# Two-layer convolution kernel: statistics of the third image moved into the first bands of both layers, weights loaded one by one, stores split, inner convolution in one piece

## Chip, cores and metric

The kernel runs on one core of one Trainium2 chip. The metric is the device time of one launch in microseconds. The kernel before took 3856.01 us, the median of three runs (3853.47 to 3856.48).

## What is computed

The input x is 8 images of 256 channels and 64 x 64 pixels, float32. Two layers follow each other, each adding its result to x after a group normalisation over 32 groups:

```
def _gn(v, G=32, eps=1e-5):
    g = v.reshape(B_, G, C_ // G, H_, W_)
    m = jnp.mean(g, axis=(2, 3, 4), keepdims=True)
    s = jnp.var(g, axis=(2, 3, 4), keepdims=True)
    return ((g - m) / jnp.sqrt(s + eps)).reshape(v.shape)
...
    x = x + _L0_conv_ref(_gn(x), ...)
    x = x + _L1_conv_ref(_gn(x), ...)
```

Layer 0 makes, for each pixel, nine tap weights per group of 8 channels, and applies them to a 3 x 3 window of a third map:

```
x1, x2, x3 = conv1x1(x, w1, b1), conv1x1(x, w2, b2), conv1x1(x, w3, b3)     # 32, 32, 256 channels
h = concatenate([x1, unfold3(reflect_pad(x2))])                              # 320 channels
h = relu(bn2(conv1x1(relu(bn1(h)), cw1)))                                    # 32 channels
w = conv1x1(h, cw2, cb2)                                                     # 9 taps x 32 groups
out = einsum('bgskhw,bgkhw->bgshw', unfold3(pad(x3)), w)
```

Layer 1 is the sum of two branches at half weight each. The first is attention of every pixel over its 7 x 7 neighbourhood, with four heads and a position term. The second takes nine depthwise 3 x 3 convolutions, a ReLU and nine more, and sums them with softmax weights over nine maps that a 256 x 2304 matrix (Wfc) makes.

## The kernel before, in words

An image is cut into 8 bands of 8 rows, so there are 64 bands, and 256 channels are two channel tiles of 128 partitions. The two layers are pipelined over bands: layer 0 is AHEAD = 12 bands ahead of layer 1. One loop runs g from -12 to 63. Each g has 8 steps s, and each step calls `advance()` six times. `after(n, f)` emits f n advances later. No scheduler reorders anything: the order in which the instructions are emitted is the order of each engine's queue, and every engine works through its queue in order. A DMA is issued by the queue of SP or ACT, in order with what else stands there.

Layer 0 of one band goes like this.

- The statistics of raw x are taken in `first_stats` (L279): a load of the band into tile xs (L100, one buffer, SP queue) and two bn_stats on VectorE (L287). This runs AHEAD0 = 21 bands ahead of layer 1. When an image's eight bands are done, `scaled_weights` (L292) forms the affine chain: aggregate, group means by a matmul (L242), sc_a on ScalarE (L146, L147), weights scaled (L300, L301), bi_a on VectorE (L273), bias by a matmul (L308).
- `small_maps` (matmul L332) and `write_maps` (ScalarE L347, L351) make x1 and x2 with three shifted copies; GpSimd adds the borders (L357 to L366). `value_maps` (matmul L375, ScalarE L380, store L382) makes x3 and stores it to DRAM; `values_by_group` loads it by group into x3q (L396 to L404, SP queue).
- `hidden_maps`: three activations write hid (L424), three sets of matmuls sum them (L434), and ReLU gives h2n (L441). In bands of g < 0 one accumulation is used. In bands of g >= 0 the matmuls come in two pieces: two thirds at step 4, a copy to h2n by ScalarE, the last third at step 6, an addition by VectorE (L450), and ReLU.
- `tap_weights`: matmul pw (L470); VectorE multiplies one tap with the shifted window into prod (L483); GpSimd adds prod to xg (L491). For g < -1 the taps come in groups of three, of which TensorE sums the third products with an identity matrix (L504), so that GpSimd has six additions per band, and VectorE's `combine` (L511) adds that sum. For g >= -1 GpSimd does all nine additions. xg starts as x, loaded by `x_by_group` (L412).
- `take` (L519) takes the statistics that layer 1 needs, and `keep` (L529) stores the band to DRAM in four DMAs: on ACT's queue when layer 0 runs alone (L525), on SP's otherwise.

Layer 1 of one band (g >= 0) loads rows with halo (L563 to L567), normalises (L572), makes values, queries and keys (L601, L684, L706), stores and reloads values by window (vd, vt; L621 to L643), makes scores (L750), softmax (L764 to L781), transposes (L787), and weighted values (L799). The other branch runs depthwise taps on VectorE (L843, L869) with ScalarE ends (L834, L879), and the matmuls pf (L886) with the exponential ex (L891). GpSimd sums the exponentials (L1106). `dynamic_sum` (L893) adds the two halves (L899), applies a limit (L902), VectorE takes the reciprocal (L907), and GpSimd multiplies: tot by rec (L908), oc by tot (L913), and adds to xr, which is stored as the output. The tile oc is written by ScalarE (L879) in `depthwise_end` and has two buffers.

The weights of layer 1 (c2 for pw is among them in the list) are all issued in one go by `layer1_loads` (L191) on ACT's queue between 23 and 28 us: wq, wk, wv, wfc (2 MB), mask, last. Afterwards VectorE scales wv (L200) and subtracts the ninth map's matrix from the other eight in two operations of 2048 columns (L205), called at three times that the main block sets.

Of the kernel before, what the change touches and what calls it, by code (L numbers as in the profile page):

```python
# [10 lines left out]
F32 = mybir.dt.float32  # L11
# [7 lines left out]
P = 128  # L19
# [68 lines left out]
def conv_layers_kernel(ctx: ExitStack, tc: tile.TileContext, ins: dict, out: bass.AP):  # L88
# [14 lines left out]
        return t  # L103


    late = []

    def load(name, shape, src=None, now=True):
        t = const.tile(shape, F32, name=f"c_{name}")
        late.append(lambda: nc.scalar.dma_start(out=t, in_=ins[name] if src is None else src))  # L110
        if now:
            late.pop()()
        return t

    nc.scalar.preload_act_table_set(TABLES)
# [6 lines left out]
    c1 = load("c1", [P, 3, REL])  # L122
    gq = load("gq", [P, P])
    gc = load("gc", [P, NCT, P])
    c2 = load("c2", [P, KK, P], now=False)
    wq = load("wq", [P, NCT, C], ins["wq"].rearrange("(t p) n -> p t n", p=P), now=False)
    wk = load("wk", [P, NCT, C], ins["wk"].rearrange("(t p) n -> p t n", p=P), now=False)
    wv = load("wv", [P, NCT, C], ins["wv"].rearrange("(t p) n -> p t n", p=P), now=False)
    wfc_in = ins["wfc"].rearrange("(t p) k n -> p t k n", p=P)
    wfc = load("wfc", [P, NCT, KK - 1, C], wfc_in[:, :, : KK - 1], now=False)  # L130

    ident = const.tile([P, P], F32, name="ident")
    make_identity(nc, ident)
# [57 lines left out]
    def layer1_loads():  # L191


        last = w1.tile([P, NCT, 1, C], F32, tag="oc", name="last")
        for f in late:
            f()
        nc.scalar.dma_start(out=last, in_=wfc_in[:, :, KK - 1 :])

        def first():
            nc.vector.tensor_scalar(wv, wv, rate1, None, ALU.mult)  # L200

        def difference(kt):
            nc.vector.tensor_sub(wfc[:, kt], wfc[:, kt], last[:, kt].to_broadcast([P, KK - 1, C]))  # L205

        return [first, lambda: difference(0), lambda: difference(1)]

    class Image:
        def __init__(self):  # L210
# [9 lines left out]
    def after(n, f):  # L220
        later.append((place[0] + n, f))
# [118 lines left out]
    def write_maps(b, i, p12, half):  # L340
        im = images[b]
        t, bias = im.x2[i], im.bias
        for u in half:
            r, o = u * R // 2, 64 * u
            for q, (dst, src) in enumerate(((1, 0), (0, 0), (0, 1))):
                n = W - (q != 1)
                nc.scalar.activation(  # L347
                    t[32 * q : 32 * q + 32, r + 1 : r + 1 + R // 2, dst : dst + n],
                    p12[o : o + 32, :, src : src + n], AF.Identity, bias=bias[o : o + 32, 0:1],
                )  # L350
            nc.scalar.activation(  # L351
                t[96:128, r : r + R // 2, :], p12[o + 32 : o + 64], AF.Identity, bias=bias[o + 32 : o + 64, 0:1]
            )
        if half[-1] == 0:
            return

        nc.gpsimd.tensor_copy(t[0:32, 1 : 1 + R, 0:1], t[0:32, 1 : 1 + R, 2:3])  # L357
        nc.gpsimd.tensor_copy(t[64:96, 1 : 1 + R, W - 1 : W], t[64:96, 1 : 1 + R, W - 3 : W - 2])

        if i == 0:  # L360
            nc.gpsimd.tensor_copy(t[0:96, 0, :], t[0:96, 2, :])
        else:
            nc.gpsimd.tensor_copy(t[0:96, 0, :], im.x2[i - 1][0:96, R, :])
            nc.gpsimd.tensor_copy(im.x2[i - 1][0:96, R + 1, :], t[0:96, 1, :])
        if i == NB - 1:
            nc.gpsimd.tensor_copy(t[0:96, R + 1, :], t[0:96, R - 1, :])  # L366
# [46 lines left out]
    def hidden_maps(b, i, alone):  # L413

        im = images[b]
        hids = []
        h2 = h2n[i % 2][:, :, :W]

        def hidden(t):
            n = P if t == 0 else 96
            hid = w0.tile([P, R, W], F32, tag="hid", name=f"hid_{b}_{i}_{t}", bufs=2)
            nc.scalar.activation(  # L424
                hid[:n], im.x2[i][:n, t : t + R, :], AF.Relu, bias=bn1b[:n, t : t + 1], scale=bn1s[:n, t : t + 1]
            )
            hids.append(hid)

        def conv(home, first, last, start, stop):
            ph = home[:, 2 * P : 3 * P].rearrange("p (r c) -> p r c", r=SR)  # L430
            for t in range(first, last):
                n = P if t == 0 else 96
                for q in range(NQR):
                    nc.tensor.matmul(  # L434
                        ph[q * REL : (q + 1) * REL], c1[:n, t], hids[t][:n, q * SR : (q + 1) * SR],
                        start=(t == start), stop=(t == stop),
                    )
            return ph

        def relu(v):  # L440
            nc.scalar.activation(h2, v, AF.Relu, bias=bn2b, scale=bn2s)  # L441

        def one(home):
            ph = conv(home, 0, 2, 0, 1)
            after(1, lambda: hidden(2))
            after(2, lambda: nc.scalar.copy(h2, ph))

        def two(home):
            ph = conv(home, 2, 3, 2, 2)
            after(1, lambda: nc.vector.tensor_add(h2, ph, h2))  # L450
            after(3, lambda: relu(h2))

        hidden(0)
        after(3 if alone else 5, lambda: hidden(1))
        if alone:

            home = ps.tile([P, 4 * P], F32, tag="acc", name=f"ph_{b}_{i}")
            after(7, lambda: conv(home, 0, 2, 0, 2))
            after(8, lambda: hidden(2))
            after(12, lambda: after(4, lambda ph=conv(home, 2, 3, 0, 2): relu(ph)))  # L460
        return [two, one]

    def tap_weights(b, i, u, alone, at):

# [48 lines left out]
        def take():  # L513
            x = im.xg[i]
            if i == 0:
                im.st1 = stat.tile([P, 2 * NB, 6], F32, tag="st1", name=f"st1_{b}")
            for t in range(2):
                v = x[:, t * SHARE // 2 : (t + 1) * SHARE // 2].rearrange("p s r c -> p (s r c)")
                nc.vector.bn_stats(im.st1[:, 2 * i + t, :], v)  # L519
            im.x1[i] = dram.tile([C, BAND], F32, tag="x1", name=f"x1_{b}_{i}")  # L520
            if alone:
                after(9, lambda: keep(nc.scalar))
            else:
                keep(nc.sync)

        def keep(queue):
            for q in range(NQR):
                v = im.xg[i][q * REL : (q + 1) * REL].rearrange("p s r c -> p s (r c)")
                queue.dma_start(out=pieces(im.x1[i], q), in_=v)  # L529

# [344 lines left out]

    def depthwise_end(b, i, ct, acc):

        oc = w1.tile([P, BAND], F32, tag="oc", name=f"oc_{b}_{i}_{ct}")
        nc.scalar.activation(oc, acc.rearrange("p r c -> p (r c)"), AF.Copy, scale=rate2)  # L879
        return oc  # L880

# [11 lines left out]
    def dynamic_sum(b, i, ct, ex, oc):  # L893

        tot = w1.tile([P, BAND], F32, tag="tots", name=f"tot_{b}_{i}_{ct}", bufs=1)
        xr = images[b].xr[i]

        engine = nc.vector if (b, i, ct) == (B - 1, NB - 1, NCT - 1) else nc.gpsimd
        engine.tensor_add(tot, ex[:, 1], ex[:, 0])  # L899


        engine.tensor_scalar(tot, tot, 1.0, 1.0e37, ALU.add, ALU.min)  # L902
        rec = w1.tile([P, BAND // 2], F32, tag="rec", name=f"rec_{b}_{i}_{ct}", bufs=1)

        def quotient(u):
            v = tot[:, u * BAND // 2 : (u + 1) * BAND // 2]
            nc.vector.reciprocal(rec, v)  # L907
            after(1, lambda: engine.tensor_mul(v, v, rec))  # L908

        def weigh():  # L910

            engine.tensor_mul(oc, oc, tot)
            engine.tensor_add(xr[:, ct], xr[:, ct], oc)  # L913
            if ct == NCT - 1:
                after(6, store)

        def store():
            nc.sync.dma_start(
                out=out[b].rearrange("(t p) n -> p t n", p=P)[:, :, i * BAND : (i + 1) * BAND], in_=xr
            )  # L920

        after(9, lambda: quotient(0))
        after(13, lambda: quotient(1))
        after(15, weigh)


    def beside(g, s):
# [73 lines left out]
    def steer(g, s):  # L1001
# [22 lines left out]
    with tc.manual_schedule():  # L1024
# [14 lines left out]
        scaled_weights(0)  # L1039
        for _ in range(32):  # L1040
            advance()
        for n, f in enumerate(layer1_loads()):
            after(4 * STEPS * (3 + n), f)

        pending, before, conv, convs, maps = [], None, None, [], []
        for g in range(-AHEAD, B * NB):
            b, i = divmod(g, NB)
            for s in range(STEPS):
# [5 lines left out]
                if g >= 0:  # L1054
                    nm = f"{b}_{i}_{ct}_{m}"
                    weighted = []
                    if m % 2 == 0:
# [154 lines left out]
```

## Time and profile before

| | |
|---|---|
| profiled execution | 3854.63 us |
| its span, first to last instruction | 3852.8 us |
| median of three runs | 3856.01 us |
| granted TensorE clock, mean | 0.994 |
| TensorE busy | 3756.3 us (97%) |
| VectorE, GpSimd, ScalarE busy | 3434.4 (89%), 3116.8 (81%), 2809.2 us (73%) |
| first score matmul of layer 1 (L750) | at 233.62 us |
| combine (L511) of the first and the ninth band | at 67.89 and 210.52 us |
| busy time per 56.3 us band in mid-run, VectorE, GpSimd, ScalarE | about 52.1, 49, 42.5 us |

The table has two times for a whole run: the profiled execution is one run, and its span leaves out what lies around the first and the last instruction. Engines are named PE (TensorE), PEld (its weight loads), DVE (VectorE), ACT (ScalarE), POOL (GpSimd) and SP; a name with q is the engine's queue while it issues or waits for DMAs. In a row of the timeline the first number is the start, the second the time to the end of the last instruction of the row, x3 says that three like instructions are drawn together, and a bracket says how long the engine was idle before and what ended that. In a row of waits the numbers are the sum in us, how many times, and the longest.

### The profile page before, as it was taken

The page shows a single profiled execution, that of the slowest core. Times are in us where ns is not written, and L with a number is a line of the kernel's source. Part 1 is how long each engine was busy: PE and PEld are TensorE (multiplying, and loading weights), DVE is VectorE, ACT ScalarE, POOL GpSimd, SP SyncE. Part 2 cuts the span into 40 slices and gives each one's busy share as a digit, 9 for nine tenths or more (in the row PEclk, how much of TensorE's full clock was granted, in tenths as well). Part 3 has the DMA queues.
Part 4 walks back from the last instruction along what each step waited for, and adds up shares of the span by engine and source line. Part 5 has one row for each costly group of instructions (what it writes and reads, how often), then busy time and mean ns, then how long its engine had stood idle before and what let it go on. Part 6 is the DMA issues. An engine that isn't in the chain of part 4 may idle for free.

```text
span 3852.8 us, 71646 instructions
## 1 busy us (share of the span) xinstructions
PE 3756.3 (97%) x24620; PEld 2109.9 (55%) x24620; DVE 3434.4 (89%) x7125; ACT 2809.2 (73%) x6770; POOL 3116.8 (81%) x2100
## 2 busy tenths in 40 slices
PE   6889999999999999999999999999999999999998
PEld 3445555555555555555555555555555555555554
DVE  6879999999999999899998999999999899978877
ACT  4457777777777777777777777777777777677776
POOL 4868888888897888888888888888888888855565
PEclk9999999999999999999999999999999999999999
DMA  8764544544444544544544544454544544232221
GB/s 247 210 177 128 142 118 129 151 126 118 133 135 131 145 123 115 148 135 127 136 116 142 142 125 120 126 149 125 136 115 117 138 119 114 74 97 78 79 67 37
DMA packets 438926, 490.14 MB, mean 127 GB/s; under 512 B 62016, under 2 KB 324256, under 8 KB 438304
## 3 DMA queue, kind: packets, MB, share of 16 engines
q1 hardware_dynamic: 421984, 469.79, 44.1%
q10 hardware_dynamic: 16576, 15.76, 1.3%
q8 instruction: 194, 3.18, 0.4%
q14 instruction: 172, 1.41, 0.1%
HBM read 343.76 MB, written 145.10 MB: 127 GB/s over the span
## 4 chain that ended last, share of the span: by engine, by line
PE 81%; POOL 10%; DVE 3%; DMA 2%; ACT 2%; issue 2%; SPq 1%; ACTq 0%; POOLq 0%; DVEq 0%
PE pf L886 39%; PE small L799 6%; PE ptp L787 6%; POOL xg L491 6%; PE pk L706 5%; PE pq L684 5%; PE sco L750 5%; PE p L375 5%; PE pv L601 5%; PE pw L470 2%; POOL ex L1106 2%; PE small L332 1%; DVE prod L483 1%; PE small L434 1%; DMA x<-x3n 1%
## 5 line engine op out<-in xcount | busy, mean ns | idle before, releaser
L886 PE MATMUL pf<-yp,c_wfc 128*128 128x512 f32 x4096 | 1916.8, 594 | 11.3 <-DVE prod L483 6.3
L491 POOL TENSOR_TENSOR xg<-xg,prod 128x1024 f32<-128x1024 f32 x549 | 1199.8, 2185 | 132.5 <-DVE prod L483 103.6
L886 PEld LDWEIGHTS pf<-yp,c_wfc 128*128 128x128 f32 x4096 | 739.6, 190 | 711.4 <-issue 654.7
L1106 POOL TENSOR_TENSOR ex<-ex,ex 128x1024 f32<-128x1024 f32 x384 | 908.8, 2367 | 68.5 <-ACT ex L891 65.0
L891 ACT ACTIVATE ex<-pf 128x512 f32<-128x512 f32 x1024 | 604.0, 590 | 347.9 <-PE pf L886 269.2
L843 DVE SCALAR_TENSOR_TENSOR acc<-yp,c_chan,acc 128x504 f32<-128x504 f32 (+3 forms) x1104 | 775.5, 702 | 63.2 <-ACT acc L834 42.8
L483 DVE SCALAR_TENSOR_TENSOR prod<-pw,c_par,x3q 128x1040 f32<-128x1040 f32 x576 | 732.7, 1294 | 107.9 <-PE pw L470 60.8
L869 DVE SCALAR_TENSOR_TENSOR acc<-hid,c_chan,acc 128x504 f32<-128x504 f32 (+3 forms) x1024 | 751.1, 733 | 18.1
L781 ACT ACTIVATE prob<-prob,tot 128x196 f32<-128x196 f32 x1024 | 412.9, 452 | 242.4 <-DVE tot L779 236.8
L772 ACT ACTIVATE prob<-prob,nmax 128x196 f32<-128x196 f32 x1024 | 458.2, 450 | 101.3 <-DVE nmax L764 101.2
L907 DVE RECIPROCAL rec<-tot 128x256 f32<-128x256 f32 x256 | 445.7, 1741 | 28.3 <-POOL tot L902 27.5
L789 ACT COPY pt<-ptp 112x512 f32<-112x512 f32 x511 | 295.9, 579 | 111.8 <-PE ptp L787 111.8
L764 DVE CUSTOM_DVE_ANT_0 prob<-sco,c_mask 128x196 f32<-128x196 f32 x1024 | 324.8, 355 | 31.0 <-PE sco L750 31.0
L787 PEld LDWEIGHTS ptp<-ident,prob 128*112 128x112 f32 x2044 | 227.3, 133 | 184.4 <-issue 132.7
L787 PE MATMUL ptp<-ident,prob 128*112 128x128 f32 x2044 | 319.5, 279 | 0.0
L908 POOL TENSOR_TENSOR tot<-tot,rec 128x256 f32<-128x256 f32 x254 | 185.8, 732 | 145.7 <-DVE rec L907 139.7
L799 PEld LDWEIGHTS small<-pt,vt 112*64 112x64 f32 x8144 | 258.6, 138 | 79.8 <-issue 60.5
L799 PE MATMUL small<-pt,vt 112*64 112x64 f32 x8144 | 294.2, 225 | 3.3 <-DMA vt<-vd 1.8
L601 PE MATMUL pv<-c_wv,yp 128*128 128x256 f32 x1056 | 253.5, 383 | 1.8 <-ACT yp L572 1.8
L902 POOL TENSOR_SCALAR tot<-tot 128x512 f32<-128x512 f32 x127 | 243.9, 1920 | 11.1
L470 PEld LDWEIGHTS pw<-h2n,c_c 128*128 128x128 f32 x1152 | 175.1, 191 | 139.9 <-issue 115.9
L375 PE MATMUL p<-xc,w3s 128*128 128x512 f32 x512 | 243.3, 598 | 0.0
(136 smaller groups left out, 4656.7 us busy)
## 6 DMA issues: line engine op xcount, KB each, us to landing
vt<-vd SPq DMA_DIRECT2D x512, 112.0 KB
x3q<-x SPq DMA_DIRECT2D x128, 264.0 KB
xc<-in_x SPq DMA_DIRECT2D x64, 512.0 KB
xg<-in_xg SPq DMA_DIRECT2D x64, 512.0 KB
yp<-x SPq DMA_DIRECT2D x128, 256.0 KB
xr<-x SPq DMA_DIRECT2D x64, 512.0 KB
out_x<-xr SPq DMA_DIRECT2D x64, 512.0 KB
xs<-in_x SPq DMA_DIRECT2D x57, 512.0 KB
```

Source lines behind the costliest of these rows:

```text
L483: nc.vector.scalar_tensor_tensor(prod[:, :, :RUN], pw[:, j, :RUN].unsqueeze(1).to_broadcast([P, SHARE, RUN]), par[:, PCB2 + k : PCB2 + k + 1],
L491: nc.gpsimd.tensor_add(im.xg[i], im.xg[i], rows(prod))
L601: nc.tensor.matmul(pv[:, g], yp[:, kt, r : r + 2].rearrange("p r c -> p (r c)"), wv[:, kt], start=(kt == 0), stop=(kt == NCT - 1),)
L772: nc.scalar.activation(prob[:, h, :NKEY], prob[:, h, :NKEY], AF.Exp, bias=nmax[:, h : h + 1], scale=-1.0, accum_out=tot[:, h : h + 1],)
L787: nc.tensor.transpose(ptp[:, h, ch], prob[:, h, ch * CHUNK : (ch + 1) * CHUNK], ident)
L799: nc.tensor.matmul(po[half[h], :, t * TQ : (t + 1) * TQ], im.vt[i + ch, m][:n, t, (2 * ct + h) * HD : (2 * ct + h + 1) * HD], pt[:n, h, ch ...
L843: nc.vector.scalar_tensor_tensor(o, yp[:, ct, ra + dr : rb + dr, ca + dc : cb + dc], chan[:, ct, CW1 + k : CW1 + k + 1], o, ALU.mult, ALU.add,
L869: nc.vector.scalar_tensor_tensor(o, hid[:, ra + dr : rb + dr, ca + dc : cb + dc], chan[:, ct, CW2 + k : CW2 + k + 1], o, ALU.mult, ALU.add,)
L886: nc.tensor.matmul(pf, wfc[:, kt, 2 * m + j, ct * P : (ct + 1) * P], images[b].yp[i][:, kt, PAD : PAD + R], start=(kt == 0), stop=(kt == N ...
L891: nc.scalar.activation(ex[:, j].rearrange("p (r c) -> p r c", r=R), pf, AF.Exp)
L907: nc.vector.reciprocal(rec, v)
L1106: after(4, lambda ex=ex, exb=exb: nc.gpsimd.tensor_add(ex, ex, exb))
```

## The change

Seven edits come together.

1. The third image's x statistics are no longer taken one band at a time for g = -5 to 2. They are taken at steps 1, 4 and 7 of g = 0, 1 and 2. For g < -10 the statistics stand at step 6 instead of 3.
2. Layer 1's loads move to SP's queue and are issued one by one over the bands g = -10 to -5 (wfc in four pieces); c2 is loaded with the first constants on ACT. The scaling of wv and the two differences move to later bands.
3. When layer 0 is alone, two of the four stores of `keep` are issued by SP, two by ACT.
4. For the first two bands of the first image, the second half of the small maps is written by VectorE rather than ScalarE, and the first two value maps are both made at step 1.
5. In bands with g >= 0 the inner convolution is one accumulation at step 6, with ReLU directly from PSUM; the copy and the addition go. hid has three buffers rather than two.
6. oc, and the tile `last` that shares its tag, have one buffer rather than two.
7. In the last band of an image, first channel tile, the limit of `dynamic_sum` is emitted five advances later, so one addition of prod to xg stands ahead of it on GpSimd, and the quotients follow later.

```diff
-        late.append(lambda: nc.scalar.dma_start(out=t, in_=ins[name] if src is None else src))
         if now:
-            late.pop()()
+            nc.scalar.dma_start(out=t, in_=ins[name] if src is None else src)
+        else:
+            late[name] = lambda: nc.sync.dma_start(out=t, in_=ins[name] if src is None else src)
...
-    c2 = load("c2", [P, KK, P], now=False)
+    c2 = load("c2", [P, KK, P])
...
+        def piece(n):
+            kt, k = n // 2, slice(n % 2 * (KK // 2), (n % 2 + 1) * (KK // 2))
+            nc.sync.dma_start(out=wfc[:, kt, k], in_=wfc_in[:, kt, k])
...
-        return [first, lambda: difference(0), lambda: difference(1)]
+        return [
+            (2, late["wq"]), (2, late["wk"]), (3, late["wv"]), (3, late["mask"]),
+            (4, lambda: piece(0)), (5, lambda: piece(1)), (6, lambda: piece(2)), (7, lambda: piece(3)),
+            (6, lambda: nc.sync.dma_start(out=last, in_=wfc_in[:, :, KK - 1 :])),
+            (5, scaled), (8, lambda: difference(0)), (9, lambda: difference(1)),
+        ]
...
+            def put(to, v, o, n):
+                if u and b == 0 and i < 2:
+                    nc.vector.tensor_scalar(to, v, bias[o : o + n, 0:1], None, ALU.add)
+                else:
+                    nc.scalar.activation(to, v, AF.Identity, bias=bias[o : o + n, 0:1])
...
-            hid = w0.tile([P, R, W], F32, tag="hid", name=f"hid_{b}_{i}_{t}", bufs=2)
+            hid = w0.tile([P, R, W], F32, tag="hid", name=f"hid_{b}_{i}_{t}", bufs=3)
...
-        def one(home):
-            ph = conv(home, 0, 2, 0, 1)
-            after(1, lambda: hidden(2))
-            after(2, lambda: nc.scalar.copy(h2, ph))
-
-        def two(home):
-            ph = conv(home, 2, 3, 2, 2)
-            after(1, lambda: nc.vector.tensor_add(h2, ph, h2))
-            after(3, lambda: relu(h2))
+        def inner(home):
+            ph = conv(home, 0, 3, 0, 2)
+            after(1, lambda: relu(ph))
...
+        else:
+            after(14, lambda: hidden(2))
+        return [inner]
...
-                after(9, lambda: keep(nc.scalar))
+                after(9, lambda: keep((nc.scalar, nc.scalar, nc.sync, nc.sync)))
...
-        oc = w1.tile([P, BAND], F32, tag="oc", name=f"oc_{b}_{i}_{ct}")
+        oc = w1.tile([P, BAND], F32, tag="oc", name=f"oc_{b}_{i}_{ct}", bufs=1)
...
+        late = 2 if (i, ct) == (NB - 1, 0) else 0
+        if late:
+            after(5, limit)
+        else:
+            limit()
...
-        after(9, lambda: quotient(0))
-        after(13, lambda: quotient(1))
-        after(15, weigh)
+        after(9 + late, lambda: quotient(0))
+        after(13 + late // 2, lambda: quotient(1))
+        after(15 + late // 2, weigh)
...
+            first = g < 2 - AHEAD
-            if s == (2 if alone else 0):
+            if s == (1 if first else 2 if alone else 0):
...
-            if s == (3 if alone else 1):
+            if s == (1 if first else 3 if alone else 1):
...
-        if s == (3 if g < -1 else 7) and g + AHEAD0 < B * NB:
-            first_stats(*divmod(g + AHEAD0, NB), n=40 if g < -1 else 9)
+        at = (6,) if g < 2 - AHEAD else (3,) if g < -1 else (1, 4, 7) if 0 <= g < 3 else (7,)
+        if s in at and not (g < 0 and g + AHEAD0 >= 2 * NB) and g + AHEAD0 < B * NB:
+            n = 2 * NB + 3 * g + at.index(s) if 0 <= g < 3 else g + AHEAD0
+            if n < 3 * NB or g >= 3:
+                first_stats(*divmod(n, NB), n=40 if g < -1 else 9)
...
-        for n, f in enumerate(layer1_loads()):
-            after(4 * STEPS * (3 + n), f)
+        for n, f in layer1_loads():
+            after(6 * STEPS * n - 9, f)
...
-                        if s in (4, 6) and convs:
+                        if s == 6 and convs:
```

More of the change, by code (lines that the diff above doesn't have):

```diff
@@ L103, in load_x @@
         return t
-    late = []
+    late = {}
     def load(name, shape, src=None, now=True):
         t = const.tile(shape, F32, name=f"c_{name}")
-        late.append(lambda: nc.scalar.dma_start(out=t, in_=ins[name] if src is None else src))
         if now:
-            late.pop()()
+            nc.scalar.dma_start(out=t, in_=ins[name] if src is None else src)
+        else:
+            late[name] = lambda: nc.sync.dma_start(out=t, in_=ins[name] if src is None else src)
         return t
@@ L129, in conv_layers_kernel @@
     wfc_in = ins["wfc"].rearrange("(t p) k n -> p t k n", p=P)
-    wfc = load("wfc", [P, NCT, KK - 1, C], wfc_in[:, :, : KK - 1], now=False)
+    wfc = const.tile([P, NCT, KK - 1, C], F32, name="c_wfc")
     ident = const.tile([P, P], F32, name="ident")
@@ L191, in layer1_loads, with scaled @@
     def layer1_loads():
[L194 to L199, printed above, removed]
+        last = w1.tile([P, NCT, 1, C], F32, tag="oc", name="last", bufs=1)
+        def piece(n):
+            kt, k = n // 2, slice(n % 2 * (KK // 2), (n % 2 + 1) * (KK // 2))
+            nc.sync.dma_start(out=wfc[:, kt, k], in_=wfc_in[:, kt, k])
+        def scaled():
             nc.vector.tensor_scalar(wv, wv, rate1, None, ALU.mult)
@@ L344, in write_maps @@
             r, o = u * R // 2, 64 * u
+            def put(to, v, o, n):
[3 more added lines that the diff above has]
+                    nc.scalar.activation(to, v, AF.Identity, bias=bias[o : o + n, 0:1])
             for q, (dst, src) in enumerate(((1, 0), (0, 0), (0, 1))):
                 n = W - (q != 1)
-                nc.scalar.activation(
+                put(
                     t[32 * q : 32 * q + 32, r + 1 : r + 1 + R // 2, dst : dst + n],
-                    p12[o : o + 32, :, src : src + n], AF.Identity, bias=bias[o : o + 32, 0:1],
+                    p12[o : o + 32, :, src : src + n], o, 32,
                 )
-            nc.scalar.activation(
-                t[96:128, r : r + R // 2, :], p12[o + 32 : o + 64], AF.Identity, bias=bias[o + 32 : o + 64, 0:1]
-            )
+            put(t[96:128, r : r + R // 2, :], p12[o + 32 : o + 64], o + 32, 32)
         if half[-1] == 0:
@@ L460, in hidden_maps @@
             after(12, lambda: after(4, lambda ph=conv(home, 2, 3, 0, 2): relu(ph)))
-        return [two, one]
+        else:
+            after(14, lambda: hidden(2))
+        return [inner]
     def tap_weights(b, i, u, alone, at):
@@ L521, in take, with keep @@
             if alone:
-                after(9, lambda: keep(nc.scalar))
+                after(9, lambda: keep((nc.scalar, nc.scalar, nc.sync, nc.sync)))
             else:
-                keep(nc.sync)
-        def keep(queue):
-            for q in range(NQR):
+                keep((nc.sync,) * NQR)
+        def keep(queues):
+            for q, queue in enumerate(queues):
                 v = im.xg[i][q * REL : (q + 1) * REL].rearrange("p s r c -> p s (r c)")
@@ L899, in dynamic_sum, with limit @@
         engine.tensor_add(tot, ex[:, 1], ex[:, 0])
-        engine.tensor_scalar(tot, tot, 1.0, 1.0e37, ALU.add, ALU.min)
+        def limit():
+            engine.tensor_scalar(tot, tot, 1.0, 1.0e37, ALU.add, ALU.min)
+        late = 2 if (i, ct) == (NB - 1, 0) else 0
[3 more added lines that the diff above has]
+            limit()
         rec = w1.tile([P, BAND // 2], F32, tag="rec", name=f"rec_{b}_{i}_{ct}", bufs=1)
```

## The prediction

> **What bounds the kernel now.** I read the page's busy row and slices first, then the busy time by stretch, then PE's waits, then the timeline of one loop of the stage before layer 1 starts.
>
> ```profile
> PE 3756.3 (97%) x24620; PEld 2109.9 (55%) x24620; DVE 3434.4 (89%) x7125; ACT 2809.2 (73%) x6770; POOL 3116.8 (81%) x2100
> PE   6889999999999999999999999999999999999998
> ```
> ```profile
> 0.00:50.00 50.00, 22.30 (x94) 11.98 (x95) 19.24 (x52) 19.43 (x42) 5.26 (x22) 0.93 0.80 271
> 50.00:100.00 50.00, 39.70 (x206) 19.48 (x205) 45.73 (x39) 22.14 (x40) 38.48 (x28) 0.97 0.82 223
> 100.00:150.00 50.00, 40.08 (x211) 20.57 (x210) 42.31 (x53) 23.20 (x45) 39.64 (x31) 0.94 0.82 224
> 300.00:350.00 50.00, 50.00 (x311) 28.15 (x310) 46.00 (x87) 38.99 (x93) 43.81 (x30) 1.00 0.47 130
> ```
> The columns after the length are busy PE, PEld, DVE, ACT and POOL, then the granted clock, DMA share and GB/s. PE lacks 3852.8 - 3756.3 = 96.5 us in all, and 67 of them lie in the first 300 us: the fill, in which layer 0 runs ahead alone. From 300 us on PE is full. So a gain has two places: a shorter fill, and some 30 us of gaps in bands and tail.
>
> ```profile
> PE ph L434 <- ACT hid L424: 20.5, 13, 2.9
> PE sco_sum L504 <- DVE prod L483: 12.0, 8, 2.7
> PE pf L886 <- DVE prod L483: 6.3, 6, 1.1
> ```
> The first two are the fill's; the third is a gap at each of six image changes. What the fill's loop itself hangs on is in DVE and POOL:
>
> ```profile
> 102.80 1.23 DVE L511 TENSOR_TENSOR xg<-sco_sum,xg 128x1024 f32<-128x1024 f32 x1 [0.66 <-POOL xg L491]
> 104.06 1.29 DVE L519 BATCH_NORM_STATS2 st<-xg 128x6 f32<-128x512 f32 x2
> 105.26 6.15 DVE L483 SCALAR_TENSOR_TENSOR prod<-pw,c_par,x3q 128x1040 f32<-128x1040 f32 x5
> 113.08 3.72 DVE L483 SCALAR_TENSOR_TENSOR prod<-pw,c_par,x3q 128x1040 f32<-128x1040 f32 x3 [1.67 <-PE pw L470]
> 116.72 1.28 DVE L287 BATCH_NORM_STATS2 st<-xs 128x6 f32<-128x512 f32 x2
> ```
> ```profile
> 107.90 11.24 POOL L491 TENSOR_TENSOR xg<-xg,prod 128x1024 f32<-128x1024 f32 x5 [2.14 <-DVE prod L483]
> ```
> From combine to combine is 16.4 us: 5.10 until POOL gets its product (combine 1.23, its statistics 1.29, two products), then five adds, 11.24. The first_stats pair (L287, 1.28) comes after POOL's products are queued, and DVE still waits 0.66 + 1.67 = 2.3 us in the loop. It is beside the path.
>
> **The change part by part.** The sum is against the profiled execution: 3854.6 us, span 3852.8, 1.8 around it. The median shown, 3856.0, is 1.4 above it; the difference is applied to the median.
>
> *Statistics out of layer 0 alone.* Five pairs (1.28 each), their loads on SP and 2.6 MB leave: 0 by the loop above, at most 5 x 1.28 = 6.4 where DVE is the late one. I take 0. One load fewer stands ahead of the first value windows (vt, L643), for which PE waited until 253.71: one SP issue, 0.65.
>
> *Statistics into bands 0 to 2.* Eight pairs where three were: 5 x 1.28 = 6.4 us more DVE in three bands, where a 56.3 us band has 52.1 of DVE. Between 0 (4.2 us free per band) and +6.4; I take +2, since two of three bands can hide theirs. Their loads go on SP ahead of vt and yp loads at 0.4 us each; DMA share there is 0.58, taken as 0.
>
> *Layer 1's weights, one by one on SP rather than at once on ACT.* Before, the load of xg at 34.47 took 8.43 us beside 3.6 MB of them, which held ACT's queue to 42.98 and the first product to 48.65. Without it the chain (maps, hidden, pw) runs as in the next band: product at about 44.6, -4.0. Bounds 0 and -5. c2 (0.6 MB) now loads early beside image 0's x, on which DVE waits: +1.2, from 0 to +2, by its share of bytes at 271 GB/s (0.6 MB takes 2.1 us). The ten issues on SP, at 0.35 to 0.75 each, lie in bands where SP waits for other things anyway: 0; their price without cover is in rival B.
>
> *The two differences (L205)* leave the first two loops:
>
> ```profile
> 55.60 4.20 DVE L205 TENSOR_TENSOR c_wfc<-c_wfc,last 128x2048 f32<-128x2048 f32 x1
> 59.73 4.95 DVE L483 SCALAR_TENSOR_TENSOR prod<-pw,c_par,x3q 128x1040 f32<-128x1040 f32 x4
> ```
> ```profile
> 61.16 6.69 POOL L491 TENSOR_TENSOR xg<-xg,prod 128x1024 f32<-128x1024 f32 x3 [3.50 <-DVE prod L483]
> 75.19 11.23 POOL L491 TENSOR_TENSOR xg<-xg,prod 128x1024 f32<-128x1024 f32 x5 [4.36 <-DVE prod L483]
> ```
> Queued behind them were the products POOL waited for: -3.5 in the first loop, less 0.9 for an L287 pair now there; 4.36 - 2.15 of a common loop = -2.2 in the second. They come back five and six loops later: mean 3.24 each (4.20 and 2.28). The first lands in image 1's affine loop, where DVE waits 2.4 for ACT's sc_a, held by four stores: with two stores on SP that wait goes, +3.24 - 2.4 = +0.8. The second meets the 2.3 us of DVE waits: +0.9. PE's next wait is again sco_sum for a product.
>
> *Fill loop so far:* -4.0 + 1.2 - 3.5 + 0.9 - 2.2 + 0.8 + 0.9 = -5.9.
>
> *Stores split.* In the last band before layer 1:
>
> ```profile
> 218.77 0.59 ACTq L529 DMA_DIRECT2D x<-xg  x1
> 219.39 1.96 ACTq L529 DMA_DIRECT2D x<-xg  x3
> 221.45 0.81 ACT L424 ACTIVATE hid<-x,bn1b,bn1s 96x512 f32<-96x512 f32 x1 [1.24 <-issue]
> ```
> PE then idles 2.77 us for that hid (ph at 222.32). Two issues at 0.65 leave ACT: -1.3. In the Trainium skill, "DMA: Bandwidth & Descriptors", section "Issuing engines are not separate DMA queues", transfers interleave on the same DMA engines whoever issued them, and a second issuer saves only the time of issuing, usually small beside the transfer. By the rule's bandwidth the split is worth 0; by the row the issuing itself is what hid stands behind. I take -1.3 here and 0 in the other bands, where ACT's waits for these stores (26.7 us in 6) lie under POOL's adds. The two on SP now wait for combine ahead of the next loads: 0, or rival B.
>
> *First maps shared, inner conv, hid.* Four small map writes of the first two bands go to DVE, idle there (9.63 us before 41.57): in the -4.0. The inner conv drops an ACT copy (0.25) and a DVE add (0.28) in each of 53 bands, PE's matmuls being the same. The Trainium skill, "Perfetto Trace Analysis", section "Identifying the Most-Contended Engine", says that matmul busy time does not show how near TensorE is to its peak and names LDWEIGHTS busy instead; that is 55% here. By it, bands would be bound by DVE (92%) and 53 x 0.28 = -15. But starts of PE's rows stand end to end:
>
> ```profile
> 681.92 1.88 PE L886 MATMUL pf<-yp,c_wfc 128*128 128x512 f32 x4
> 683.64 0.39 PE L470 MATMUL pw<-h2n,c_c 128*128 128x132 f32 x2
> ```
> Four pf take 1.72 us from start to next start, and such spacings fill the band. The measurement decides: 0.
>
> *late.* At an image's last band POOL's limit (L902, 1.92 us at 682.38) stood ahead of the add that frees a prod buffer; DVE's product then came at 686.60 and PE's pf waited 1.07 at 687.96. With one add first the product comes 1.9 earlier and the wait goes: 6.3 us in six. Bounds 0 and -6.3; -6.3 taken. rec, which waits for limit instead, is late by 2.2 and next in line, with DVE work queued behind it.
>
> *oc with one buffer.* A new wait: ACT's write (L879) must wait for POOL's multiply (L913) of the channel tile before. At one band L913 ends at 1047.15 and the next write starts at 1048.59: slack 1.4 us; the other tile has 3.1. 0; price in rival C. Behind that write on ACT stand ex (L891) and prob, and PE waits for both.
>
> **Sum:** -5.9 - 0.65 - 1.3 + 2 - 6.3 = -12.1, so 3856.0 - 12.1 = 3843.9.
>
> **Rivals.** *A*, as summed, 3838 to 3850: 48%.
> *B*, SP becomes the late queue. Ten more issues and two waiting stores per band stand ahead of the x3q loads; SP already waits 47.7 us in 10 for x3n and 47.6 in 8 for xs. If products come 1 us later in six loops, +6; and stats at their full 6.4 rather than 2, +4.4: 3854.3. For it: ordered queue, waits ahead. Against: x3q is fetched a loop ahead. 26%.
> *C*, slower: oc's single buffer. One POOL add more (2.18) ahead of L913 exceeds the 1.4 us of slack by 0.8; over 64 bands 51 us, of which ACT, idle 13.8 us of a band's 56.3, passes half to PE: 3843.9 + 26 = 3870. It decides once L913 is late by over 1.4 us in common bands. For it: thin slack. Against: nothing in the change delays POOL outside band 7. 14%.
> *D*, DVE is the late one in the fill (the combine at 119.17 shows no wait for POOL): -6.4 more, and stats in bands for nothing, -2: 3835.5. 12%. This also covers the title's part doing alone what it says.
>
> **Numbers.** Less than 0.2% (7.7 us) can't be told from no change. Faster (under 3848.3): A and D, 0.60; same: B, 0.26; slower: C, 0.14. Leaving out C and D's end gives 3833 to 3862.
>
> **What would show it.** Combine starts some 5 us earlier at the first and 6 at the ninth; loops of 16.4 us unchanged in between; L205 near image 1's bias; first score near 226; the pf wait for prod gone at image changes; no wait of ACT for POOL at L879. A loop shorter than 16 us means D; longer SP waits ahead of x3q mean B; ACT acc or oc waiting for POOL means C. Wrong altogether if DVE's statistics in bands 0 to 2 open PE gaps over 6 us.

## The result, and the profile after

The changed kernel takes 3871.2 us (median of six runs, 3868.4 to 3879.0) where the kernel before took 3854.7 in the same comparison. The ratio is 1.0045, 95% interval 1.0033 to 1.0056: 17 us slower, where 12 us faster was predicted. The profiled execution took 3869.04 us. Its span, from the first to the last instruction, is 3866.8: 14.0 more than before. Line numbers of the changed kernel are 5 to 17 higher: pf is L892, ex L897, the sum of exponentials L1123, product L489, combine L517, the store L535.

First the page of the changed kernel, busy row and TensorE's slices, then two stretches of its busy time, in the columns of before.

```profile
PE 3762.0 (97%) x24620; PEld 2113.1 (55%) x24620; DVE 3426.9 (89%) x7080; ACT 2801.1 (72%) x6709; POOL 3118.4 (81%) x2100
PE   6889999999999999999999999999999999999998
```
```profile
100.00:150.00 50.00, 40.26 (x209) 21.22 (x208) 41.91 (x51) 21.28 (x40) 37.89 (x30) 0.92 0.92 246
300.00:350.00 50.00, 49.69 (x342) 28.51 (x339) 47.88 (x94) 39.74 (x95) 43.39 (x29) 1.00 0.51 146
```
VectorE and ScalarE have 7.5 and 8.1 us less work, and the kernel is slower all the same. (The counts fit the edits: 53 additions gone from VectorE and 8 map writes come, so 45 fewer; 53 copies and 8 writes gone from ScalarE, so 61 fewer.) Two things differ. In the fill the DMA engines are busier between 100 and 150 us (0.92 instead of 0.82), with no more done by VectorE or GpSimd. And between 300 and 350 us TensorE isn't full: 49.69 of 50. The fill was to end some 6 us earlier and ends 1.0 later: the first score matmul starts at 234.60 instead of 233.62, and the first and the ninth combine at 68.61 and 214.13 instead of 67.89 and 210.52. The waits of TensorE, whole run; the last line is from the kernel before:

```profile
PE sco_sum L510 <- DVE prod L489: 20.2, 11, 5.1
PE pf L892 <- ACT ex L897: 16.0, 37, 1.0
PE ph L444 <- ACT hid L434: 7.3, 5, 3.9
```
```profile
PE pf L886 <- ACT ex L891: 4.4, 10, 1.1
```
The pf waits for prod at six image changes are gone, as predicted. In their place pf waits for ACT's ex 37 times, 16.0 us where it was 4.4 in 10. The hid waits of the fill fell by 13 us, and the sco_sum waits rose by 8.

A page shows such a loss badly, since it is spread thin. What shows it is the start of the same instruction, band by band, in both traces. The table gives the start of the oc write (ScalarE, one per band taken) less its start in the profiled execution before, in us; these differences are called marks below. The last row is the difference of the whole spans. The later columns are the experiments below.

| band | changed | e1 two pieces | e2 step 4 | e3 before + inner | e4 before + late | e9 kept parts | e12 one add less |
|---|---|---|---|---|---|---|---|
| 0 | +1.4 | +4.2 | +1.8 | +0.7 | 0.0 | -6.4 | +6.1 |
| 1 | +3.3 | +6.2 | +4.0 | +1.2 | +0.3 | -4.3 | +8.0 |
| 7 | +3.4 | +5.7 | +3.0 | +2.7 | +0.2 | -5.1 | +5.8 |
| 8 | +2.8 | +4.4 | +1.2 | +3.2 | -1.0 | -6.9 | +4.8 |
| 15 | +5.2 | +4.7 | +0.5 | +5.7 | -1.0 | -7.6 | +3.8 |
| 16 | +4.2 | +3.5 | -1.1 | +5.7 | -2.3 | -9.2 | +2.4 |
| 51 | +11.6 | -1.5 | -11.0 | +16.8 | -7.6 | -19.1 | -7.6 |
| 63 | +11.3 | -1.4 | -11.7 | +16.5 | -7.6 | -19.7 | -10.1 |
| span | +14.0 | +1.3 | -9.0 | +16.5 | -4.7 | -17.0 | -7.3 |

The changed kernel has lost 3.3 us by band 1 and stands there until the first image change. From band 8 on it loses about 0.45 us in six bands of eight, gets 1.0 back at each image change (0.6 at the first), and loses nothing between bands 51 and 63, where layer 0 has no more work. The span adds 2.7 behind the last oc write; e4 will show where from. One losing band, in TensorE's timeline, before and after (the same piece of work, 9.0 to 9.5 us later in the changed kernel):

```profile
2696.53 0.65 PE L434 MATMUL small<-hid,c_c 128*32 128x128 f32 x16
2697.11 0.65 PE L787 MATMUL ptp<-ident,prob 128*112 128x128 f32 x4
...
2705.36 1.89 PE L601 MATMUL pv<-c_wv,yp 128*128 128x256 f32 x8
2707.09 1.88 PE L886 MATMUL pf<-yp,c_wfc 128*128 128x512 f32 x4
2708.81 0.39 PE L470 MATMUL pw<-h2n,c_c 128*128 128x132 f32 x2
...
2711.06 0.43 PE L434 MATMUL small<-hid,c_c 96*32 96x128 f32 x8
2711.41 0.65 PE L787 MATMUL ptp<-ident,prob 128*112 128x128 f32 x4
```
```profile
2706.07 0.65 PE L793 MATMUL ptp<-ident,prob 128*112 128x128 f32 x4
...
2714.32 1.89 PE L607 MATMUL pv<-c_wv,yp 128*128 128x256 f32 x8
2716.53 1.98 PE L892 MATMUL pf<-yp,c_wfc 128*128 128x512 f32 x4 [0.31 <-ACT ex L897]
2718.35 0.39 PE L476 MATMUL pw<-h2n,c_c 128*128 128x132 f32 x2
...
2720.60 0.87 PE L444 MATMUL small<-hid,c_c 128*32 128x128 f32 x24
2721.39 0.65 PE L793 MATMUL ptp<-ident,prob 128*112 128x128 f32 x4
```
Before, 16 matmuls of the inner convolution (0.58 us from start to next start) stand at step 4, ahead of this stretch. In the changed kernel they are gone from there and come with the rest at step 6, after it. So TensorE reaches the pf sooner, and waits 0.31 us there. From start to start the gap costs more than the bracket says: pv to pf takes 2.21 instead of 1.73, and pf to pw 1.82 instead of 1.72. That is 0.58 us, all that had been taken away ahead of it. At step 6 the 24 matmuls take 0.79 us where the 8 took 0.35, so the band is 0.44 longer. (Apart, the 16 and the 8 took 0.93 together: in one row the same matmuls take 0.14 us less.) What pf waits for is in ScalarE's timeline, before and after, and in GpSimd's of the changed kernel:

```profile
2706.34 0.60 ACT L891 ACTIVATE ex<-pf 128x512 f32<-128x512 f32 x1 [1.91 <-POOL ex L1106]
```
```profile
2715.88 0.60 ACT L897 ACTIVATE ex<-pf 128x512 f32<-128x512 f32 x1 [2.48 <-POOL ex L1123]
```
```profile
2709.09 4.44 POOL L497 TENSOR_TENSOR xg<-xg,prod 128x1024 f32<-128x1024 f32 x2
2713.48 2.36 POOL L1123 TENSOR_TENSOR ex<-ex,ex 128x1024 f32<-128x1024 f32 x1
```
GpSimd runs back to back: two additions of products, then the sum of two ex tiles, which frees an ex tile at 2715.84. Only then can ScalarE write the next ex and so free a PSUM tile for pf. GpSimd's rows are those of before, 9.54 us later, while TensorE's pv comes only 8.96 later. Before, too, the ex waited 1.91 us for GpSimd; it ended at 2706.94, and pf followed at 2707.09 without a gap. So work that TensorE does ahead of that point is free as long as it fills the time until GpSimd is done, and work moved behind it is paid for.

### The profile page after: what moved, and what is told of

The parts are those of the page before. It is cut to its first block, busy times and chain, and to the rows that moved or that the text cites. A ratio compares the mean times of both kernels' runs of the same rounds, so it can differ in the third digit from the quotient of the medians.

```text
span 3866.8 us, 71657 instructions
## 1 busy us (share of the span) xinstructions
PE 3762.0 (97%) x24620; PEld 2113.1 (55%) x24620; DVE 3426.9 (89%) x7080; ACT 2801.1 (72%) x6709; POOL 3118.4 (81%) x2100
## 3 DMA queue, kind: packets, MB, share of 16 engines
q14 instruction: 172, 1.41, 0.1%
## 4 chain that ended last, share of the span: by engine, by line
PE 62%; POOL 22%; DVE 7%; ACT 3%; issue 3%; DMA 2%; SPq 0%; ACTq 0%; POOLq 0%; DVEq 0%
PE pf L892 30%; POOL xg L497 12%; POOL ex L1123 7%; PE small L805 5%; PE p L385 4%; PE sco L756 4%; PE ptp L793 4%; PE pq L690 4%; PE pk L712 3%; DVE prod L489 3%; PE pv L607 2%; PE small L337 1%; POOL oc L925 1%; PE pw L476 1%; PE small L444 1%
## 5 line engine op out<-in xcount | busy, mean ns | idle before, releaser
L892 PE MATMUL pf<-yp,c_wfc 128*128 128x512 f32 x4096 | 1920.0, 595 | 17.3 <-ACT ex L897 16.0
L892 PEld LDWEIGHTS pf<-yp,c_wfc 128*128 128x128 f32 x4096 | 739.1, 190 | 726.1 <-issue 658.8
L1123 POOL TENSOR_TENSOR ex<-ex,ex 128x1024 f32<-128x1024 f32 x384 | 908.4, 2366 | 59.4 <-ACT ex L897 55.4
L897 ACT ACTIVATE ex<-pf 128x512 f32<-128x512 f32 x1024 | 605.4, 591 | 381.3 <-PE pf L892 275.1
L489 DVE SCALAR_TENSOR_TENSOR prod<-pw,c_par,x3q 128x1040 f32<-128x1040 f32 x576 | 732.5, 1294 | 110.8 <-PE pw L476 47.5
L355 ACT ACTIVATE x<-small,bias 32x252 f32<-32x252 f32 x504 | 233.2, 463 | 46.2 <-PE small L337 39.1
```

The lines of the kernel that those rows point to most:

```text
L489: nc.vector.scalar_tensor_tensor(prod[:, :, :RUN], pw[:, j, :RUN].unsqueeze(1).to_broadcast([P, SHARE, RUN]), par[:, PCB2 + k : PCB2 + k + 1],
L892: nc.tensor.matmul(pf, wfc[:, kt, 2 * m + j, ct * P : (ct + 1) * P], images[b].yp[i][:, kt, PAD : PAD + R], start=(kt == 0), stop=(kt == N ...
L897: nc.scalar.activation(ex[:, j].rearrange("p (r c) -> p r c", r=R), pf, AF.Exp)
L1123: after(4, lambda ex=ex, exb=exb: nc.gpsimd.tensor_add(ex, ex, exb))
```

## The experiments

Differences in us are the ratio less one, times 3854.7.

**e1: two pieces again.** The changed kernel with the old inner convolution; oc keeps one buffer, hid three.

```diff
-        else:
-            after(14, lambda: hidden(2))
-        return [inner]
+        return [two, one]
...
-                        if s == 6 and convs:
+                        if s in (4, 6) and convs:
```

> The changed kernel with the inner convolution in two pieces again (steps 4 and 6, copy and addition back); everything else as changed, oc with one buffer too. Theory, order of TensorE's work: in the changed kernel 0.62 us of TensorE work (16 matmuls) moved from ahead of a pf that waits for a POOL-freed ex buffer to behind it, and some 38 bands lose 0.45 us. Then this kernel is about 17 us faster than the changed one (3854), its bands are 56.85 us again where they were 57.3, and the waits of pf for ACT ex fall from 16 us back to about 4. Rival, single oc buffer: nothing is gained, bands stay at 57.3 and the time near 3871. Rival, statistics in bands 0 to 2: same, nothing gained.

Measured: 3854.0 us, ratio to before 1.0002 (0.9993 to 1.0011). TensorE's wait:

```profile
PE pf L896 <- ACT ex L901: 5.0, 12, 1.1
```
All 17 us are back. From band 3 on the marks stand still between image changes (5.7 at bands 3 and 7, 4.7 at 9 and 15), with one oc buffer: that rival is out, and so are the statistics as a cost in every band. The late edit shows as 1.2 to 1.3 gained at each image change.

**e2: one piece at step 4.**

```diff
-            after(14, lambda: hidden(2))
+            after(11, lambda: hidden(2))
...
-                        if s == 6 and convs:
+                        if s == 4 and convs:
```

> The changed kernel with the whole inner convolution at step 4 instead of step 6 (third hidden map three advances earlier). Theory, order: all 24 matmuls now stand ahead of the pf that waits for the ex buffer, so the 0.45 us per band goes and the time is about 3854. Rival, that one accumulation or the direct ReLU itself costs: bands stay at 57.3, time near 3871. In between, if the earlier hidden map delays ex on ACT.

Measured: 3846.1 us, ratio 0.9980 (0.9973 to 0.9988); pf waits 3.4 us for ex, in 10. So neither the single accumulation nor the direct ReLU costs anything: their place did. It is 8 us better than e1, more than was expected. The busy time of TensorE says why, first e1, then e2:

```profile
PE 3758.6 (98%) x24620; PEld 2111.5 (55%) x24620; DVE 3438.6 (89%) x7133; ACT 2803.3 (73%) x6762; POOL 3118.0 (81%) x2100
PE 3750.9 (98%) x24620; PEld 2114.2 (55%) x24620; DVE 3427.3 (89%) x7080; ACT 2790.7 (73%) x6709; POOL 3117.8 (81%) x2100
```
The same 24620 matmuls take 7.7 us less. Over 53 bands that is the 0.14 us by which 24 inner matmuls in one row are shorter than 16 and 8 apart, and the marks of e2 fall by 0.14 in most bands.

**e3: the kernel before with only the inner convolution in one piece at step 6** (the same diff as in the change, with hid at three buffers and oc at one).

> The kernel before with only the inner convolution in one piece at step 6, hid with three buffers and oc with one (which makes the room). Theory, order: +0.45 us in about 38 bands, +17 us, 3872; the fill as before (first score at 233.6). Rival, that the loss of the changed kernel comes from its fill and statistics: within 2 us of before.

Measured: 3869.3 us, ratio 1.0038 (1.0023 to 1.0053), +14.6 us. Its wait is the changed kernel's:

```profile
PE pf L882 <- ACT ex L887: 15.5, 37, 1.0
```

**e4: the kernel before with only the late limit** (the two pieces of the change's diff that have `late`).

> The kernel before with only the limit of the last band's dynamic sum moved behind one addition. Theory: the pf wait for prod at six image changes (1.07 each) goes, and the marks of the changed kernel drop by 1.0 + 0.45 there: -6 to -9 us, 3846 to 3849. Rival: the wait is taken over by ACT ex or by rec, 0 to -2 us.

Measured: 3849.6 us, ratio 0.9988 (0.9981 to 0.9994), -4.6 us. In the profiled execution the marks drop six times by 1.3, 7.6 in all. The span is only 4.7 shorter, since 2.9 us are given back behind the last mark. All six kernels of the table with this edit give back 2.7 to 2.9 there, and e3, which lacks it, nothing. The edit delays the limit in the last band of every image, the eighth too, where no next image follows. That this delay is what comes back there is the likely reading; it was not tested apart.

**e5 to e8: one part each of what acts in the fill, on the kernel before.** e5 has the weights one by one on SP with c2 early and the differences later; e6 has

```diff
-                after(9, lambda: keep(nc.scalar))
+                after(9, lambda: keep((nc.scalar, nc.scalar, nc.sync, nc.sync)))
```
e7 has the statistics at g = 0 to 2 instead of -5 to 2, and e8 the shared first maps.

> The kernel before with only layer 1's weights loaded one by one on SP (c2 early on ACT) and the differences later. Prediction's step: first combine about 5 us earlier, ninth about 6 earlier, -6 us in all. Rival, SP's queue and the early c2 take it back: TensorE starts 2 to 2.6 us later (mv_a near 22.9), the x3q loads land later, ninth combine within 2 us of before or later, 0 to +4 us in all.

> The kernel before with only the alone stores split between ACT and SP. Prediction's step: ACT's wait of 26.7 us for these stores shrinks, loops unchanged, -1.3 us in the last band ahead of layer 1. Rival, SP waits for combine ahead of xg and x3q loads (in the changed kernel 41.1 us in 8, up to 9.5): products come later, loops of 17 to 18 us rather than 16.4, +3 to +8 us.

> The kernel before with only the third image's statistics moved into bands 0 to 2. Prediction's step: fill loops unchanged, -0.65 at the first value windows, +2 in bands 0 to 2: about +1 us. Rival one: SP is freed of its waits for tile xs (48.9 us in 9) and x3q comes earlier, loops shorten by 0.5 or more, -3 us. Rival two: eight statistics in three bands cost their full 6.4 us.

> The kernel before with only the first maps shared between ScalarE and VectorE and the first two value maps at one step. Prediction's step: first product earlier by up to 2 us. Rival: VectorE's half starts only when ScalarE's is done (32.53 after 32.50 in the changed kernel), so nothing is gained and the fill stays within 1 us.

| part | ratio (interval) | us | combines 1 and 9 start at (before 67.9, 210.5) |
|---|---|---|---|
| e5 loads | 1.0020 (1.0011 to 1.0029) | +7.7 | 70.0, 222.1 |
| e6 stores | 0.9991 (0.9983 to 1.0000) | -3.5 | 67.0, 209.3 |
| e7 statistics | 1.0000 (0.9992 to 1.0009) | 0.0 | 67.0, 206.2 |
| e8 maps | 1.0007 (1.0000 to 1.0014) | +2.7 | 71.0, 218.2 |

Profiles of e7 and e8 lie further out (-4 and +7 at the last band) than their medians: the fill is what varies from one execution to the next. In e7 bands 0 to 3 lose 1.5 us (-5.5 to -4.0). In e8 the two engines don't share the time: VectorE's half starts when ScalarE's ends (30.87 after 30.83). The rows are from the changed kernel, where the same edit stands.

```profile
30.60 1.90 ACT L355 ACTIVATE x<-small,bias 32x252 f32<-32x252 f32 x4 [3.34 <-PE small L337]
```
```profile
32.53 2.00 DVE L353 TENSOR_SCALAR x<-small,bias 32x252 f32<-32x252 f32 x4 [3.56 <-PE p L385]
```

**e9: the parts that gained, together.** Before, with one piece at step 4, late, stores split, statistics moved; weights and first maps as before.

> The kernel before with the parts that gained: inner convolution in one piece at step 4 (hid three buffers, oc one), late, stores split, statistics of the third image in bands 0 to 2. If parts add up: two pieces to one at step 4 is 7.9 (e2 against e1), late 4.4, stores 2.4, statistics 1.3, so 3854.6 - 16 = 3838.6. Rival, the fill's parts don't add, since stores on SP and statistics relieve the same queue: 3842 or more.

Measured: 3839.6 us (3836.4 to 3841.4), ratio 0.9958 (0.9946 to 0.9971): 16 us faster than before, 31 to 32 faster than the changed kernel. That is within 1 us of the sum that was expected.

**e10: e5 with the weights issued by ACT's queue.**

```diff
-            late[name] = lambda: nc.sync.dma_start(out=t, in_=ins[name] if src is None else src)
+            late[name] = lambda: nc.scalar.dma_start(out=t, in_=ins[name] if src is None else src)
```
(and likewise for wfc's pieces and last).

> The kernel before with the weights loaded one by one over the same bands, but issued by ACT's queue rather than SP's. Theory one, SP's queue is what the loads delay: the 7.4 us of the loads part go, 3854 or less, and no wait of a product for x3q or for weights. Theory two, the loads collide with the fill's other transfers on the DMA engines (share 0.82 before): the loss stays, 3859 to 3863.

Measured: 3855.7 us, ratio 1.0002 (0.9994 to 1.0011). The loss of e5 is gone. VectorE's waits for loads ahead of a product in the fill, first e5, then e10:

```profile
DVE prod L488 <- DMA x3q<-x: 7.5, 1, 7.5
DVE prod L488 <- DMA c_wv<-in_wv: 5.3, 1, 5.3
```
```profile
DVE prod L488 <- DMA x3q<-x: 2.0, 1, 2.0
```
The second row names c_wv, but the product doesn't read that tile: VectorE scales wv only at 95.1. What the product reads is x3q, and the last x3q load of its band stands on SP just ahead of c_wv, issued at 63.76 in e5 and at 60.25 in e10.

The same bytes for the same bands, at a DMA share of 0.82 from 50 to 200 us (e5: 0.78), cost nothing that can be told from zero when ACT's queue issues them. So what costs is that SP issues them, and not their bytes. How it comes to cost is not fully shown. On ACT they also start earlier (c_wq at 44.99 instead of 48.43, c_wv at 56.99 instead of 64.41), and between 50 and 62 us one wait of SP for a stored x3n takes 8.2 us in e5, where e10's longest is 4.0. Standing ahead on SP and transfers that meet at another moment were not separated, nor which of the ten issues costs how much.

**e11: only the differences moved.** The loads stay as before; the times of the two differences are those of the change.

> The kernel before with only the two differences moved to the later bands, loads as before. Prediction's step: first combine 3.5 earlier, second interval 2.2 shorter, given back 0.8 and 0.9 four loops later: -4 us. Rival, given back in full (3.2 each) later: 0.

Measured: 3854.3 us, ratio 1.0001 (0.9993 to 1.0010). The first combine comes at 66.2 and the second loop (to the second combine) falls from 18.56 to 16.34, as in the step; but loops four to nine take 17.3, 17.7, 23.3, 18.9, 17.2 and 20.4 instead of 16.4, 16.4, 21.9, 16.9, 16.7 and 19.4, and the ninth combine comes at 213.7. All is given back.

**e12: one addition less on GpSimd.** The changed kernel, without tap 5's addition in bands of g >= -1.

```diff
-            else:
+            elif alone or k != 5:
                 nc.gpsimd.tensor_add(im.xg[i], im.xg[i], rows(prod))
```

> The changed kernel, leaving out one of the nine additions of products in every band where both layers run (tap 5 is missing from the sum), the one ahead of GpSimd's sum of exponentials in step 5. Theory, pf waits for an ex buffer that GpSimd frees late: the wait of pf for ex falls from 16 us to under 4 and the bands lose their 0.45 us, so 3854 or less. Rival, the order costs TensorE its time whatever GpSimd does: near 3871.

Measured: 3844.5 us, ratio 0.9971 (0.9960 to 0.9982). The wait is nearly gone although TensorE's order is the changed kernel's:

```profile
PE pf L892 <- ACT ex L897: 1.2, 4, 0.3
```
So GpSimd's place in the chain is shown: with one addition less on it, TensorE keeps its order and loses its wait. That is 28 us less than the changed kernel by the ratios, where 17 was expected:

```profile
PE 3751.1 (98%) x24620; PEld 2116.9 (55%) x24620; DVE 3419.9 (89%) x7080; ACT 2796.8 (73%) x6709; POOL 2999.2 (78%) x2045
```
In the profiled executions the pf waits are 14.8 us less and TensorE's busy time is 10.9 less. The 17 was the loss that remained after the 0.14 us saved in each band. A gap itself costs 0.58 from start to start, part of it in the rows around it, and 33 gaps less make some 19 us. The marks show further gains of 0.6 in the last band of each image and 2.4 after band 51; what stands behind these is open.

## Why the prediction was wrong, point by point

**"PE's matmuls being the same" and "The measurement decides: 0" for the inner convolution.** This is the step that failed most: +14.6 measured (e3). It asked how full TensorE is and whether its work changes. That TensorE is full was read rightly. The work is not quite the same: in one row the matmuls take 0.14 us less in each band, a gain of some 7 us that the sum had at nothing (e2). The larger miss is the overlap: it didn't ask where the 16 matmuls stood against the next thing TensorE waits for from outside. In the trace of before the answer could be read: ScalarE's ex waits 1.91 us for GpSimd's sum in that band, and pf starts 0.15 us after that ex ends; in the changed kernel, where pf does wait, it starts 0.05 after. So 0.1 us was to spare. Taking 0.58 us of TensorE's work from ahead of that point opens a gap that costs all of it, and the same work is done again behind it: about 0.45 net in 35 bands of the changed kernel.

**"The ten issues on SP ... lie in bands where SP waits for other things anyway: 0."** The second failure. The loads part as a whole, with c2 and the differences, was to give -5.9 with the maps and cost +7.7 (e5). With the weights on ACT's queue the part costs 0.8 (e10), so it is the issue on SP that was mis-sized: about 7 us, not 0. SP's waits of 47.7 and 47.6 us weren't spare time, since x3q loads that products need stand behind them in the same queue. Rival B named the place rightly, at +6 for the loads; how the issues make the products late is in part open (e10).

**"Product at about 44.6, -4.0."** The first product came at 49.69, later than the 48.65 of before. TensorE started 2.6 us later, and the pw matmuls that the product needs at 47.52 instead of 46.78. Without the slow xg load the last hid activation was no longer held; the x3q load, which waits for the stored x3n, came last instead:

```profile
49.69 3.72 DVE L489 SCALAR_TENSOR_TENSOR prod<-pw,c_par,x3q 128x1040 f32<-128x1040 f32 x3 [8.15 <-DMA x3q<-x]
```
The step removed one wait and didn't follow the chain of the next: the product needs both pw and x3q. The shared maps, counted into the -4.0, cost 2.7 (0 to 5.4; e8).

**The differences, "-3.5, -2.2, +0.8, +0.9".** In e11 the first two came: from the first product to the first combine 16.8 us instead of 19.2, and 2.2 less in the second loop. The last two were undersized: all is given back, 0.4 net. In the changed kernel the first didn't come, 18.9 us, since a product waits 3.68 for an x3q load there. The two differences take 3.71 and 3.15 us in it, and the loops around them aren't the only ones that grow.

**c2, +1.2.** TensorE starts at 22.87 rather than 20.30. One profile each doesn't decide it: the eight kernels with c2 where it was start at 20.3 to 22.1, mean 21.0, the six with c2 early at 21.5 to 22.9, mean 22.2. The means differ by the 1.2 that was forecast, the ranges overlap, and what a later start costs at the end is not shown.

**Stores, -1.3, and statistics, 0 - 0.65 + 2.** Measured -3.5 (-6.6 to 0) and 0 (-3 to +3.5): right within what the runs tell. The +2 for bands 0 to 2 shows as 1.5 in e7. (The busy times used for it are those of a 56.3 us band. A band in mid-run takes 57.8 us on average, with 53.2 of VectorE, so 4.6 us are free and not 4.2.) In the last band before layer 1 of the changed kernel the stores' issue is shorter and hid waits less for it:

```profile
220.41 0.56 ACTq L535 DMA_DIRECT2D x<-xg  x1
221.00 0.62 ACTq L535 DMA_DIRECT2D x<-xg  x1
221.73 0.80 ACT L434 ACTIVATE hid<-x,bn1b,bn1s 96x512 f32<-96x512 f32 x1
```
PE's wait there is 1.41 instead of 2.77, the predicted 1.3 almost to the tenth; then waits of 1.09 and 0.76 for products stand behind it, at pk and pq. Both parts also shorten image 1's affine loop: 21.9 us before, 18.0 in e6, 17.3 in e7, 17.8 with both in e9. There they don't add. The statistics' place at step 6 for g < -10 was not tried by itself.

**late, -6.3.** Measured -4.6 (-7.3 to -2.3). The wait was read rightly, and each of six image changes gains 1.3, 7.6 in all (e1, e4). The sum left out the eighth image, whose last band gives back 2.7 to 2.9.

**oc with one buffer, 0.** Right (e1): in the changed kernel ScalarE's oc write waits for GpSimd's last reading of oc once in the whole run, 0.2 us. So rival C, whose 3870 is the measured time to 1 us, met the number by luck and was wrong in its place: ScalarE does wait for GpSimd in the common bands, but for an ex tile, not for oc.

Added up by ratios, the parts give 7.7 + 2.7 - 3.5 + 0 + 14.6 - 4.6 = 16.9 us; the changed kernel shows 17.3. The parts' intervals allow some 9 us either way, so that they meet this closely is in part luck; the bands' 14.6 and late's -4.6 are seen in the marks, the fill's parts only in their medians.

## What to carry to other kernels

When work is moved on a full engine, its amount is only half the question: look for the next point at which that engine, or the one that frees its buffers, waits for something from outside, and count what the move takes from ahead of that point. A wait of a helper engine that ends just before the full engine arrives is such a point, though the full engine shows no gap. Where work is regrouped, read its time from start to next start in both groupings; the same matmuls need not take the same time. An edit that gains at every repeat can cost at the last one, so count the ends too. And a queue that mostly waits isn't free: ask what stands behind the new issues in it.

## What the runs showed that was not expected

Moving the same 24 matmuls from step 6 to step 4 changes the kernel by 25 us (3871.2 to 3846.1). The 16 us of work saved on VectorE and ScalarE show in no run: what one piece gains (e2 against e1) is TensorE's own 7.7 us, from the same matmuls in one row. The same weight loads, over the same bands, cost 7.7 us on SP's queue and 0.8, not told from zero, on ACT's.
